# A four-layer convolution kernel: the channel mix as 64-row matmuls, and a place in the tick for each engine's part of a stage

## The chip, the core and the metric

One core of a Trainium2 chip runs the whole program. Five engines take part, each with its own queue in program order: TensorE (PE in the profile; its weight loads are the row PEld), VectorE (DVE), ScalarE (ACT), and SyncE (SP), which issues most DMA transfers; GpSimd is idle. The metric is device time in microseconds, the median of several executions. Before the change it is 2977.2 us (three runs, 2973.15 to 2978.07).

## What is computed

The input x is 4 images of 64 channels of 256 x 256, f32. Layers 0, 1 and 3 are long convolutions, written in the reference with FFTs; the filter of a channel is an outer product of a column filter and a row filter, so that the kernel does each layer as two triangular Toeplitz matmuls (along rows, then along columns) and a residual sum with a bias. Layer 2 is a Haar transform, a channel mix with thresholds, and the inverse transform:

```
k = einsum('ijk,imk->ijmk', hx, hy)            # layers 0, 1, 3: separable filters
out = irfft2(rfft2(x) * rfft2(k)) + x * bias

f1 = haar2d(x)                                  # layer 2
acc = 0
for i in range(2):
    f3 = f1 * v[i]
    f4 = einsum('bchw,oc->bohw', f3, conv_w[i]) # 64 channels to 64
    acc += sign(f4) * relu(abs(f4) - tau[i])
y = haar2d(acc, inverse=True) + x
```

## The kernel before

An image b passes through three parts, and the parts of neighbouring images overlap. `convolutions` takes a channel at a time: layer 0 and layer 1 (four products called pa and py; `contract`, L187 to L191, makes each of four matmuls), the residual sums on VectorE (L212), the pairs of the Haar transform (L257, L258), its other levels (L269, L270, four channels at once), a split of the result into two parts (L280 on ScalarE, L281 on VectorE) and a matmul for the column transform (`down`, L288), whose result ScalarE copies out (L296) and a DMA writes to DRAM as `coef`. `mixing` reads `coef` back with channels on partitions, 64 groups g for an image. `inverse` takes a channel at a time again: a copy out of z (L396), row matmuls (pw, L403, L404), a split (L406, L407), a column matmul (pu, L416), sums (L420 to L424), and layer 3. One channel in three has its layer 3 put off to the last image's mixing stage, where no channels of a next image are left (`convolution`, tile v).

What the change touches most is `mixing`. The tile f has 128 partitions: two coefficient rows r of 64 channels each. A group needs four stationary blocks of f (q and h, two each). The moving operand wb has 128 rows and 256 columns and is block-diagonal: rows 0 to 63 hold the 64 x 128 weights in columns 0 to 127, rows 64 to 127 hold them in columns 128 to 255, and the rest is zero (memset at L153, DMAs at L155). So `mix` issues 4 matmuls of 128 x 128 by 128 x 256 for a group (L340); their result px is two PSUM banks of 16 pieces of 64 columns. Each piece has a scale of its own: VectorE scales the first 16 - n_act pieces in one instruction (L357), ScalarE the other n_act with one instruction each (L359); n_act is 12, and 6 for the last image. `shrink` takes magnitude and sign on ScalarE (L365, L366) and subtracts the threshold on VectorE (L367); `signed` (L372) and `add` (L376) end the group on VectorE and write z. PSUM tiles px, and the SBUF tiles f4 and mag, have two buffers each; f has three.

The order of the work is a list of events: `at(tick, place, run, unit)`; the list is sorted by tick and place, and each event then emits its instructions. A tick has one group of `mixing`, or one channel of `inverse`. `spread` lays the 64 channels of the next image over the ticks of a mixing stage and a few before and after. A Tile scheduler then lays out each engine's queue, guided by that order.

Of the kernel before, what the change touches and what calls it, by code (L numbers as in the profile page):

```python
# [17 lines left out]
P = 128  # L18
# [3 lines left out]
BUFS = {"res": 1, "y": 3, "co": 2}  # L22

# [14 lines left out]
def conv_seq_kernel(ctx, tc, x, fz, fw, bias, decay, haar, haar_row, factors, vt, taut, wmix, out):  # L38
# [33 lines left out]
    wb = const.tile([P, 2, P], F32, name="wb")  # L72
# [3 lines left out]
    z = zpool.tile([P, 2, S, C], F32, name="z")  # L76
# [10 lines left out]
    room = z.rearrange("p h r c -> p (h r c)")  # L87
# [60 lines left out]
    def constants():  # L148
        signs = part(P)
        nc.sync.dma_start(hbt, haar[0])  # L150
        nc.sync.dma_start(signs, haar[1])
        nc.sync.dma_start(hrow, haar_row)
        nc.vector.memset(wb, 0.0)  # L153
        for r in range(2):
            nc.sync.dma_start(wb[r * C : (r + 1) * C, r, :], wmix)  # L155
        nc.scalar.copy(hb, signs)
        nc.scalar.copy(hbr, hbt)
# [35 lines left out]
    def first(b, st, key, layer, new):  # L193
        def run(c):
            s = st[c]
            ps = bank(f"p{new}_{b}_{c}")
            contract(ps, s[key], s[layer][:, 0, :])
            a = io.tile([P, 2, S], F32, name=f"{new}_{b}_{c}", tag="mid")
            nc.scalar.copy(a, ps)  # L199
            s[new] = a  # L200

        return run

    def second(b, st, key, layer, res, new, tag, ahead=None):
        def run(c):
            s = st[c]
            if ahead is not None:
                s[ahead] = toeplitz(ahead, c, f"t{ahead}_{b}_{c}")
            ps = bank(f"p{new}_{b}_{c}")
            contract(ps, s[key], s[layer][:, 1, :])  # L210
            y = io.tile([P, 2, S], F32, name=f"{new}_{b}_{c}", tag=tag, bufs=BUFS[tag])
            nc.vector.scalar_tensor_tensor(y, s[res], bsb[:, layer, c : c + 1], ps, ALU.mult, ALU.add)  # L212
            s[new] = y

        return run

    def butterfly(b):

        d = mx.tile([P, 2, C], F32, name=f"bfly_{b}", tag="mag")
        nc.vector.tensor_sub(d, z[:, :, 0, :], z[:, :, 1, :])  # L220
        nc.vector.tensor_add(z[:, :, 0, :], z[:, :, 0, :], z[:, :, 1, :])
        nc.vector.tensor_copy(z[:, :, 1, :], d)
# [5 lines left out]
    def at(tick, place, run, unit):  # L228
        events.append((tick, place, len(events), run, unit))

    def stream(stages, ticks):

        for unit, tick in enumerate(ticks):
            for s, stage in enumerate(stages):
                if stage is not None:
                    at(tick + s, -s, stage, unit)

    def convolutions(b, ticks, in_parts=(), border=None):
# [12 lines left out]
        last_second = second(b, st, "a1", 1, "y0", "y1", "res")  # L251

        def pairs(c):
            last_second(c)
# [21 lines left out]
        def split(c):  # L276

            w = parts[c] = mx.tile([P, 2, 2, S], F32R, name=f"sp_{b}_{c}", tag="sp", bufs=1)
            t = sd[:, c % 8].rearrange("p k e w -> p k (e w)")
            nc.scalar.copy(w[:, 0], t)  # L280
            nc.vector.tensor_tensor(w[:, 1], t, w[:, 0].bitcast(F32), ALU.subtract)  # L281

        def down(c):
# [7 lines left out]
            else:  # L291
                nc.tensor.matmul(
                    ps.rearrange(flat), hbt, sd[:, c % 8].rearrange("p k e w -> p (k e w)"), start=True, stop=True
                )
            t = io.tile([P, 2, S], F32, name=f"co_{b}_{c}", tag="co", bufs=BUFS["co"])
            nc.scalar.copy(t, ps)  # L296
            nc.sync.dma_start(coef[b][:, c].rearrange("k p w -> p k w"), t)

        stream(
            [load, first(b, st, "x", 0, "a0"), second(b, st, "a0", 0, "x", "y0", "y", ahead=1), first(b, st, "y0", 1, "a1"), pairs],  # L300
            ticks,
        )
        for c, tick in enumerate(ticks):

            at(tick + 4, 3, store, c)
        for n in range(C // 4):
            end = ticks[4 * n + 3] + 4
            for s, steps in enumerate([(1,), (2, 4), (8, 16, 32, 64)]):
                at(after(end + 1 + s, n), 1, levels(steps), n)
            for j in range(4):  # L310
                if 4 * n + j in in_parts:
                    at(after(end + 3 + j, n), 2, split, 4 * n + j)
                at(after(end + 4 + j, n), 2, down, 4 * n + j)
        return after(ticks[-1] + 11, C // 4 - 1)

    def mixing(b, start, n_act):
# [18 lines left out]
        def mix(g):  # L335
            f = st[g]["f"]
            ps = psx.tile([P, 2, 2, S], F32, name=f"px_{b}_{g}", tag="mix")
            for q in range(2):
                for h in range(2):
                    nc.tensor.matmul(  # L340
                        ps[:, h, q, :],
                        f[:, q, h * P : (h + 1) * P],
                        wb.rearrange("p r n -> p (r n)"),
                        start=True,
                        stop=True,
                    )
            if g == 0:

                one, two = ps[:, :, 0, :P], ps[:, :, 0, P:]
# [4 lines left out]
            f4 = mx.tile([P, 16, C], F32, name=f"f4_{b}_{g}", tag="f4")  # L354
            px = ps.rearrange("p h q (r i o) -> p (h q r i) o", r=2, i=2)
            n = 16 - n_act
            nc.vector.tensor_tensor(f4[:, :n], px[:, :n], over(g, 0, n), ALU.mult)  # L357
            for j in range(n, 16):
                nc.scalar.mul(f4[:, j], px[:, j], scale(g, 0)[:, j : j + 1])  # L359
            st[g]["f4"] = f4  # L360

        def shrink(g):
            f4 = st[g]["f4"]
            mag = mx.tile([P, 16, C], F32, name=f"mag_{b}_{g}", tag="mag")
            nc.scalar.activation(mag, f4, AF.Abs)  # L365
            nc.scalar.activation(f4, f4, AF.Sign)  # L366
            nc.vector.tensor_sub(mag, mag, over(g, 1, 16))  # L367
            st[g]["mag"] = mag
# [5 lines left out]
        def add(g):  # L374
            parts = st.pop(g)["mag"].rearrange("p (h r i) o -> p h r i o", h=2, i=2)
            nc.vector.tensor_add(z[:, :, 4 * g : 4 * g + 4, :], parts[:, :, :, 0, :], parts[:, :, :, 1, :])  # L376

        for g in range(S // 4):
            at(start + g - 2, 0, load, g)

            for s, (place, stage) in enumerate([(-2.5, mix), (-3.5, shrink), (-4.1, signed), (-4.2, add)]):
                at(start + g + s, place, stage, g)

    def inverse(b, start, put_off):
# [3 lines left out]
        def fetch(c):  # L390
# [5 lines left out]
            nc.scalar.copy(a, z[:, :, :, c].rearrange("p h (i k) -> p h k i", k=2))  # L396
            st[c] = {"r": r, "z": a}

        def rows(c):
# [5 lines left out]
            w = mx.tile([P, 2, 2, 2, P], F32R, name=f"w_{b}_{c}", tag="f4")  # L405
            nc.scalar.copy(w[:, 0], ps)  # L406
            nc.vector.tensor_tensor(w[:, 1], ps, w[:, 0].bitcast(F32), ALU.subtract)  # L407
            st[c]["w"] = w
            if c not in put_off:
                st[c][2] = toeplitz(2, c, f"t2_{b}_{c}")  # L410

        def cols(c):
            ps = psm.tile([P, 2, 2, P], F32, name=f"pu_{b}_{c}", tag="mm")
            flat = "p m e w -> p (m e w)"
            for i in range(2):
                nc.tensor.matmul(  # L416
                    ps.rearrange(flat), hb, st[c]["w"][:, i].rearrange(flat), start=(i == 0), stop=(i == 1)
                )
            t = io.tile([P, 2, 2, P], F32, name=f"t_{b}_{c}", tag="res", bufs=BUFS["res"])
# [7 lines left out]
        ends = last(b, st)  # L427
        for c in range(C):

            at(start + c, -1, fetch, c)  # L430
            at(start + c + 1, -9, rows, c)
            at(start + c + 2, -8, cols, c)
            if c in put_off:
                at(start + c + 3, -5, lambda c: nc.scalar.dma_start(late[b, c], st.pop(c)["u"]), c)
            else:
                for s, stage in enumerate(ends):
                    at(start + c + 3 + s, s - 7, stage, c)

    def last(b, st):
        return [  # L440
            first(b, st, "u", 2, "a3"),
            second(b, st, "a3", 2, "u", "y3", "co"),
# [3 lines left out]
    def convolution(which, ticks):  # L446

        for (b, c), tick in zip(which, ticks):
# [7 lines left out]
            for s, stage in enumerate([load, *last(b, st)]):  # L456
                at(tick + s, -s, stage, c)
# [21 lines left out]
    for tick, do in enumerate([constants, None, None, *three[:-1], *tables()], 4):  # L479
        if do is not None:  # L480
            at(tick, 3, lambda unit, do=do: do(), 0)
# [5 lines left out]
    for b in range(B):  # L487
        mixing(b, start, 12 if b + 1 < B else 6)
# [11 lines left out]
    for _, _, _, stage, unit in sorted(events, key=lambda e: e[:3]):  # L500
# [110 lines left out]
```

## Time and profile before

| | |
|---|---|
| median of the runs | 2977.2 us |
| the profiled execution: its time | 2975.2 us |
| its span on the core | 2973.4 us |
| busy in the span: PE, PEld | 2913.8 us (98%), 2615.1 us (88%) |
| busy in the span: DVE, ACT | 2545.5 us (86%), 2156.9 us (73%) |
| granted TensorE clock | 1.0 |
| DMA | 649.73 MB, mean 219 GB/s |

From the first to the last matmul of the mix (L340), the four mixing stages run from 453.5 to 860.1 us, 1092.1 to 1532.6, 1765.9 to 2206.2 and 2436.2 to 2707.5. Between them lie the inverse stages. Busy time is the union of an engine's instructions; a matmul's end is modelled, and matmuls overlap, so that the start-to-start times of matmuls tell their cost and not the lengths of the records. An f32 matmul appears as two records, each with a weight load of its own: the 1024 matmuls of L340 are 2048 records.

### The profile page before, as it was taken

What the parts mean: (1) busy time and instruction counts of PE and PEld (TensorE: products, weight loads), DVE (VectorE), ACT (ScalarE), POOL (GpSimd) and SP (SyncE); (2) the same over time, 40 slices, a digit from 0 to 9 for tenths busy, and PEclk for the clock granted to TensorE, in tenths of its full rate; (3) what the DMA queues carried; (4) which work ended last, traced back from release to release, by engine and by line L of the source; (5) the groups of instructions that cost most, each with busy time, mean ns of one, the idle gap of its engine ahead of it and who ended that gap; (6) DMA issues with size and microseconds to landing.
All of it is one profiled execution on the core that took longest, in us unless ns stands there. A gap on an engine that the chain in (4) does not pass through costs nothing. (4 is left out here: it accounts for less than half of the span.)

```text
span 2973.4 us, 52066 instructions
## 1 busy us (share of the span) xinstructions
PE 2913.8 (98%) x16950; PEld 2615.1 (88%) x16950; DVE 2545.5 (86%) x4571; ACT 2156.9 (73%) x5014; POOL 0.2 (0%) x4
## 2 busy tenths in 40 slices
PE   8999999999999999999999999999999999999999
PEld 6898988888888898888888988888888988888998
DVE  5766768999998879999989879999998889998776
ACT  2333338999986758889986668989986768887554
POOL 0000000000000000000000000000000000000000
PEclk9999999999999999999999999999999999999999
DMA  5877777666667876776777876777777878777676
GB/s 159 247 237 226 229 228 212 203 202 207 207 196 244 250 217 200 208 216 204 208 219 244 250 225 197 209 210 211 207 216 237 256 236 235 233 230 217 212 212 186
DMA packets 562497, 649.73 MB, mean 219 GB/s; under 512 B 44369, under 2 KB 447412, under 8 KB 562100
## 3 DMA queue, kind: packets, MB, share of 16 engines
q1 hardware_dynamic: 482996, 562.07, 64.8%
q10 hardware_dynamic: 79232, 84.34, 8.0%
q8 instruction: 137, 2.24, 0.3%
q14 instruction: 132, 1.08, 0.1%
HBM read 426.77 MB, written 219.48 MB: 217 GB/s over the span
## 5 line engine op out<-in xcount | busy, mean ns | idle before, releaser
L190 PE MATMUL py<-t,a 128*128 128x256 f32 x3072 | 919.0, 381 | 8.9 <-ACT a L199 5.5
L199 ACT COPY a<-pa 128x512 f32<-128x512 f32 x768 | 477.2, 621 | 387.9 <-PE pa L191 357.2
L359 ACT ACTIVATE f<-px,vt 128x64 f32<-128x64 f32 x2688 | 582.3, 358 | 143.5 <-DVE f L357 143.4
L191 PEld LDWEIGHTS py<-t,a 128*128 128x128 f32 x3072 | 583.4, 190 | 79.3
L191 PE MATMUL py<-t,a 128*128 128x128 f32 x3072 | 590.0, 274 | 0.0
L190 PEld LDWEIGHTS py<-t,a 128*128 128x128 f32 x3072 | 500.4, 191 | 50.9 <-ACT a L199 12.4
L340 PE MATMUL px<-wb,f 128*128 128x256 f32 x2048 | 488.2, 380 | 4.9 <-ACT f L359 4.9
L340 PEld LDWEIGHTS px<-wb,f 128*128 128x128 f32 x2048 | 369.5, 190 | 47.0 <-ACT f L359 6.7
L367 DVE TENSOR_TENSOR mag<-mag,vt 128x1024 f32<-128x1024 f32 x256 | 312.4, 1220 | 28.3 <-ACT mag L365 26.9
L190 PE MATMUL pa<-t,y 128*128 128x256 f32 x1024 | 311.6, 386 | 22.4 <-DVE y L212 20.3
L406 ACT CAST w<-pw 128x512 fp32r<-128x512 f32 x256 | 150.2, 587 | 227.0 <-PE pw L404 218.9
L372 DVE SCALAR_TENSOR_TENSOR mag<-mag,f 128x1024 f32<-128x1024 f32 x256 | 311.7, 1218 | 1.9
L190 PE MATMUL pa<-t,x 128*128 128x256 f32 x1024 | 305.9, 380 | 0.4 <-issue 0.4
L365 ACT ACTIVATE mag<-f 128x1024 f32<-128x1024 f32 x256 | 293.7, 1147 | 11.0 <-DVE z L376 8.8
L366 ACT ACTIVATE f<-f 128x1024 f32<-128x1024 f32 x256 | 285.2, 1114 | 3.0
L396 ACT COPY zc<-z 128x512 f32<-128x512 f32 x256 | 282.0, 1103 | 0.7 <-ACT w L406 0.4
L281 DVE TENSOR_TENSOR sp<-sd,sp 128x512 fp32r<-128x512 f32 x256 | 176.1, 688 | 91.4 <-ACT sp L280 90.2
L190 PE MATMUL pa<-t,u 128*128 128x256 f32 x772 | 232.8, 383 | 2.9 <-PE pu L416 1.6
L420 DVE SCALAR_TENSOR_TENSOR t<-r,pu 128x512 f32<-128x512 f32 x256 | 174.9, 683 | 60.4 <-PE pu L416 57.0
L212 DVE SCALAR_TENSOR_TENSOR y<-x,bsb,py 128x512 f32<-128x512 f32 x256 | 190.1, 742 | 37.9 <-PE py L191 36.1
L212 DVE SCALAR_TENSOR_TENSOR y<-y,bsb,py 128x512 f32<-128x512 f32 x256 | 190.0, 742 | 34.2 <-PE py L191 33.1
L191 PEld LDWEIGHTS pa<-t,x 128*128 128x128 f32 x1024 | 194.6, 190 | 26.3
(67 smaller groups left out, 4458.9 us busy)
## 6 DMA issues: line engine op xcount, KB each, us to landing
t<-pad SPq DMA_DIRECT2D x768, 256.0 KB, 3.9
x<-in_x SPq DMA_DIRECT2D x256, 256.0 KB, 3.6
keep<-sd SPq DMA_DIRECT2D x256, 256.0 KB, 2.9
coef<-co SPq DMA_DIRECT2D x256, 256.0 KB, 3.3
f<-coef SPq DMA_DIRECT2D x256, 256.0 KB, 3.2
r<-keep SPq DMA_DIRECT2D x256, 256.0 KB, 3.3
out_y<-y ACTq DMA_DIRECT2D x256, 256.0 KB, 3.6
late<-u ACTq DMA_DIRECT2D x63, 256.0 KB, 2.9
```

Source lines behind the costliest of these rows:

```text
L190: nc.tensor.matmul(ps[:, m, :], src[:, 0, m * P : (m + 1) * P], t[:, ::-1], start=True, stop=False)
L191: nc.tensor.matmul(ps[:, m, P:], src[:, 1, m * P : (m + 1) * P], t[:, : P - 1 : -1], start=False, stop=True)
L199: nc.scalar.copy(a, ps)
L212: nc.vector.scalar_tensor_tensor(y, s[res], bsb[:, layer, c : c + 1], ps, ALU.mult, ALU.add)
L281: nc.vector.tensor_tensor(w[:, 1], t, w[:, 0].bitcast(F32), ALU.subtract)
L340: nc.tensor.matmul(ps[:, h, q, :], f[:, q, h * P : (h + 1) * P], wb.rearrange("p r n -> p (r n)"), start=True, stop=True,)
L359: nc.scalar.mul(f4[:, j], px[:, j], scale(g, 0)[:, j : j + 1])
L365: nc.scalar.activation(mag, f4, AF.Abs)
L366: nc.scalar.activation(f4, f4, AF.Sign)
L367: nc.vector.tensor_sub(mag, mag, over(g, 1, 16))
L372: nc.vector.scalar_tensor_tensor(mag, mag, 0.0, st[g]["f4"], ALU.max, ALU.mult)
L396: nc.scalar.copy(a, z[:, :, :, c].rearrange("p h (i k) -> p h k i", k=2))
```

## The change

Seven things are edited.

- wb loses its zeros: it is 128 x 128, with the 64 x 128 weights twice, on partitions 0 to 63 and on 64 to 127. `mix` issues 8 matmuls for a group with 64 contraction rows and 128 moving columns, alternately on rows 0 to 63 and rows 64 to 127, the two halves into two different PSUM banks. The built program has 2048 such matmuls in place of 1024, with the tile size 64 x 128 and the tile positions (0, 0) and (64, 0).
- The pieces of px now stand in the order r, h, q, i, and the tables of scales, the layout of z, `butterfly`, `add` and the copy out of z (256 B between elements in place of 512 B) follow.
- n_act is 14 for the first image, and stays 12, 12 and 6 for the others.
- Each stage is cut by engine: a product and the copy or sum after it, `split` and `rest`, `down` and `away`, `rows` and `halves`, `cols` and `join`, and in `mixing` the scaling (VectorE's, and two halves of ScalarE's), `size`, `sign` and `shrink`.
- `at(time, run, unit)` takes one number; the table PLACE gives each part its offset from the unit's tick, with a second set (prefix l) for the last image's mixing.
- The second residual sum and the pairs of layer 1 are events of their own (4.429 and 4.639); the threshold steps (`shrink` 1.777, `signed` 2.802, `add` 3.331) get places of their own too.
- The load of f is placed 0.977 ticks before the group's tick, where it was 2 ticks before.

```diff
+N_ACT = (14, 12, 12, 6)
+PLACE = {
...
+    "y0": 2.571,
+    "y0 sum": 2.571,
...
+    "mix load": -0.977,
+    "mix": 0.536,
+    "scaled": 0.583,
+    "scaled too": 0.583,
+    "scaled rest": 0.584,
+    "size": 1.468,
+    "sign": 1.476,
+    "shrink": 1.777,
+    "signed": 2.802,
+    "add": 3.331,
...
-    wb = const.tile([P, 2, P], F32, name="wb")
+    wb = const.tile([P, P], F32, name="wb")
-    z = zpool.tile([P, 2, S, C], F32, name="z")
+    z = zpool.tile([P, 2, 2, P, C], F32, name="z")
...
-        nc.vector.memset(wb, 0.0)
         for r in range(2):
-            nc.sync.dma_start(wb[r * C : (r + 1) * C, r, :], wmix)
+            nc.sync.dma_start(wb[r * C : (r + 1) * C], wmix)
...
-    def at(tick, place, run, unit):
-        events.append((tick, place, len(events), run, unit))
+    def at(time, run, unit):
+        events.append((time, len(events), run, unit))
...
         def mix(g):
             f = st[g]["f"]
-            ps = psx.tile([P, 2, 2, S], F32, name=f"px_{b}_{g}", tag="mix")
-            for q in range(2):
-                for h in range(2):
-                    nc.tensor.matmul(
-                        ps[:, h, q, :],
-                        f[:, q, h * P : (h + 1) * P],
-                        wb.rearrange("p r n -> p (r n)"),
-                        start=True,
-                        stop=True,
-                    )
+            ps = psx.tile([P, 2, 2, 2, P], F32, name=f"px_{b}_{g}", tag="mix")
+            for h in range(2):
+                for q in range(2):
+                    for r in range(2):
+                        rows = slice(r * C, (r + 1) * C)
+                        nc.tensor.matmul(
+                            ps[:, r, h, q, :], f[rows, q, h * P : (h + 1) * P], wb[rows], start=True, stop=True
+                        )
...
-            px = ps.rearrange("p h q (r i o) -> p (h q r i) o", r=2, i=2)
+            st[g]["px"] = ps.rearrange("p r h q (i o) -> p (r h q i) o", i=2)
+
+        def scaled(g):
+            px, n = st[g]["px"], 16 - n_act
+            nc.vector.tensor_tensor(st[g]["f4"][:, :n], px[:, :n], over(g, 0, n), ALU.mult)
+
+        def scaled_too(g, half):
+            px, f4 = st[g]["px"], st[g]["f4"]
+            for j in range(16 - n_act + half * (n_act // 2), 16 - (1 - half) * (n_act - n_act // 2)):
+                nc.scalar.mul(f4[:, j], px[:, j], scale(g, 0)[:, j : j + 1])
+
+        def size(g):
+            mag = st[g]["mag"] = mx.tile([P, 16, C], F32, name=f"mag_{b}_{g}", tag="mag")
+            nc.scalar.activation(mag, st[g]["f4"], AF.Abs)
+
+        def sign(g):
+            nc.scalar.activation(st[g]["f4"], st[g]["f4"], AF.Sign)
...
-            parts = st.pop(g)["mag"].rearrange("p (h r i) o -> p h r i o", h=2, i=2)
-            nc.vector.tensor_add(z[:, :, 4 * g : 4 * g + 4, :], parts[:, :, :, 0, :], parts[:, :, :, 1, :])
+            parts = st.pop(g)["mag"].rearrange("p (s q i) o -> p s q i o", q=2, i=2)
+            rows = z.rearrange("p r h i c -> p (r h) i c")[:, :, 2 * g : 2 * g + 2, :]
+            nc.vector.tensor_add(rows, parts[:, :, :, 0, :], parts[:, :, :, 1, :])
...
-            nc.scalar.copy(a, z[:, :, :, c].rearrange("p h (i k) -> p h k i", k=2))
+            nc.scalar.copy(a, z[:, :, :, :, c].rearrange("p k h i -> p h k i"))
...
-        mixing(b, start, 12 if b + 1 < B else 6)
+        mixing(b, start, N_ACT[b])
```

## The prediction

> **What bounds the kernel now.** The page names PE as the chain's main engine, but its busy shares are means over unlike stages. So I first read the busy times cut at the stages: image 0's first convolutions, the four mixing stages (the third equals the second to 0.2 us and is left out), the last inverse stage, and a piece of the last mixing.
>
> ```profile
> core 0: us, PE busy (x) PEld busy (x) DVE busy (x) ACT busy (x) POOL busy (x), PEclk, DMA share, GB/s
> 60.00:450.00 390.00, 385.11 (x2276) 348.76 (x2275) 272.99 (x593) 146.63 (x270) 0.00 (x0) 1.00 0.78 231
> 455.00:860.00 405.00, 395.56 (x2171) 349.90 (x2171) 386.89 (x668) 374.99 (x1077) 0.00 (x0) 1.00 0.68 204
> 1092.00:1532.00 440.00, 434.27 (x2428) 389.47 (x2427) 407.76 (x716) 386.39 (x1092) 0.00 (x0) 1.00 0.71 208
> 2436.00:2707.00 271.00, 265.85 (x1434) 236.40 (x1433) 264.30 (x309) 233.17 (x554) 0.00 (x0) 1.00 0.79 234
> 2725.00:2955.00 230.00, 229.93 (x1476) 212.07 (x1475) 164.93 (x306) 135.51 (x186) 0.00 (x0) 1.00 0.69 210
> 2600.00:2650.00 50.00, 49.23 (x267) 43.89 (x267) 49.80 (x58) 45.07 (x109) 0.00 (x0) 1.00 0.80 235
> ```
>
> Outside the mixing stages PE alone is full (99 to 100%), and the change takes no matmul out there. In the mixing stages three engines are nearly full together: 98.7, 92.7 and 87.8% in the second. The waits inside that stage say which one sets the pace (engine, line, waited for: us, times, longest):
>
> ```profile
> DVE y L212 <- PE py L191: 11.3, 15, 1.2
> ...
> PE pa L190 <- DVE y L212: 4.9, 7, 1.7
> ...
> ACT f L359 <- DVE f L357: 45.9, 45, 2.5
> ```
>
> PE waits 4.9 us of 440; ScalarE waits for VectorE's scaling, VectorE for PE. The end is set by PE, with VectorE 6% behind. Last, the group rows of the mix and the order of time around one group of it, and around a start with nothing preloaded (start, us, engine, line):
>
> ```profile
> L340 PE MATMUL px<-wb,f 128*128 128x256 f32 x2048 | 488.2, 380 | 4.9 <-ACT f L359 4.9
> L357 DVE TENSOR_TENSOR f<-px,vt 128x256 f32<-128x256 f32 x192 | 80.4, 419 | 0.5 <-PE px L340 0.5
> L357 DVE TENSOR_TENSOR f<-px,vt 128x640 f32<-128x640 f32 x64 | 52.3, 817 | 1.5
> ```
>
> ```profile
> 1007.33 0.30 PEld L403 LDWEIGHTS pw<-hrow,zc 128*128 128x128 f32 x2
> ...
> 1007.67 0.30 PEld L403 LDWEIGHTS pw<-hrow,zc 128*128 128x128 f32 x2
> ...
> 1304.71 1.89 PE L340 MATMUL px<-wb,f 128*128 128x256 f32 x8
> ...
> 1306.43 0.59 PE L190 MATMUL py<-t,a 128*128 128x256 f32 x2
> ...
> 1307.49 2.56 ACT L359 ACTIVATE f<-px,vt 128x64 f32<-128x64 f32 x12 [0.38 <-DVE f L357]
> ...
> 2553.31 1.99 PE L340 MATMUL px<-wb,f 128*128 128x256 f32 x8 [0.69 <-ACT f L359]
> ```
>
> A group of the mix costs PE 1306.43 - 1304.71 = 1.72 us: 8 records of 0.215. Between the two load lines at 1007.33 and 1007.67 lie three records of 128 columns, so one costs 0.34/3 = 0.113 us, whether its load or its stream sets that.
>
> **The change, part by part.** The span has 64 groups in each of four stages. I divide by the groups each window holds (L340's records in it: 505, 509, 509, by 8: 63.1, 63.6, 63.6). Per group, in us:
> first stage: 6.42, of it PE 6.27, DVE 6.13, ACT 5.94; second and third: 6.92, of it 6.83, 6.41, 6.08; last: 4.26, of it 4.18, 4.16, 3.67.
>
> *The mix.* 16 records of 128 columns on 64 rows replace 8 of 256. The trace has no pair on two row halves, so I bound. One after another they cost 16 x 0.113 = 1.81 us. If the halves run side by side, in loads and streams both, half: 0.90. To this come the two borders of a group, where the array passes from 128-row to 64-row work and back. The least is nothing, as between L340 and L190 now. The most is a full drain and an exposed start: a record outlasts its slot by 0.380 - 0.215 = 0.165, and the mix at 2553.31, which began with its load, ran 1.99 against 1.89, 0.10 more; 0.27 a border, 0.53 a group. Side by side thus costs 0.90 to 1.43, and I take the middle, 1.17: 0.55 less than now (0.29 to 0.82). I take side by side because the built program addresses the halves separately and gives each half its own PSUM bank, so nothing that the program declares chains one half to the other.
>
> Two rules bear on this. The Trainium skill, TensorE: Matmul & The Clock Gate, section LDWEIGHTS, speaks against the change: a load's time goes by its columns and not by its rows, P/1.2 ns, so a 64-row load is no cheaper; as an estimate 16 x 107 ns = 1.71 us a group if loads queue, which by itself would cancel the gain. TensorEngine Tiling (Array Packing), Key Properties, says that different tiles load and multiply in parallel, which would give 0.86, and that a change of tiling mode drains TensorE, which is on the side of my upper border cost. The 0.113 agrees with the first for full-height loads; no run here shows the rest.
>
> *What that is worth.* In the second and third stages PE falls from 6.83 to 6.28 and VectorE's 6.41 becomes the most. How near can a group's time come to it? In the last stage, where VectorE is full already, it is busy 264.30 of 271 us, 97.5%. 6.41/0.975 = 6.57, 0.35 below 6.92; 64 groups in two stages: **-45 us**. Ends: VectorE at the 99.6% of 2600 to 2650 gives 6.44, -61; half of the gap kept in waits between ScalarE and VectorE gives -20.
>
> *n_act 14 in the first stage.* VectorE's L357 goes from 256 to 128 elements, at (817 - 419)/(640 - 256) = 1.04 ns each: -0.13, to 6.00. ScalarE gets two more instructions at (2.56 - 0.36)/11 = 0.20 each (0.36: L359's mean of 358 ns): 5.94 + 0.40 = 6.34, which is 98.8% of 6.42. So ScalarE takes PE's place, and I take **0**. Ends: ScalarE packs better and VectorE decides, 6.00/0.975 = 6.15, -17; ScalarE at 97.5%, 6.50, +5.
>
> *The last stage.* VectorE's 4.16/0.975 is today's 4.26: **0**, and -5 if it reaches 99.6% throughout.
>
> *The places.* I laid the two programs' queues side by side. In the convolution and inverse stages PE's queue, matmul by matmul, and ScalarE's read alike in the stretches I compared; VectorE's differ by a neighbour here and there. In mixing the second image's groups keep their sequence (PE: mix, py, pa, pz, py, pa; VectorE: scale, sign, sum, add, sum, split, pairs, subtract). SP's loads of f, t and v stand in the same sequence in the last mixing stage, though the table puts f's load later, so no transfer is moved past another there. So I cost the table at 0; what hides its small shifts is VectorE's slack outside mixing (272.99 of 390 us busy). If a group lost one 0.4 us instruction's wait on VectorE to it, that would be 0.4 x 128 = 51 us in the second and third stages; the like gain is inside the -61 above.
>
> *Layout of z.* The copy out of z (L396, 1103 ns) may change with its step; it lies in the inverse stages, where ScalarE is busy 133 of 202 us (59% in the last) and PE is full: 0 up or down, unless it grew by over 1.0 us of a channel's 3.2 (202 us by 64). The memset saved is 0.3 us.
>
> Sum: 2973.4 - 45 = 2928 us of span; the median runs stand 3.8 us above that span (2977.2), so **2932 us**, with 2894 (-83: -61, -17, -5) to 2962 (-15: -20, +5) as this case's own range.
>
> **Rivals.** *The halves don't run side by side* (the slower side). Place: `mix`, in the four mixing stages. Price: 1.81 plus 0 to 0.53 for 1.72, that is 0.09 to 0.62 more on PE, the engine that sets the pace (the last stage's PE is 98% busy, so it pays too): 256 x 0.09 = +23 to 256 x 0.62 = +159, so 3000 to 3136. It decides from the point where a group costs PE over 1.72 us. For it: the loads, doubled in number, have at 0.113 each no room under 0.9 us of streams. Against: separate halves and banks.
>
> *The relieved PE finds the others in its old rhythm.* ScalarE's 45.9 us of waits for the scaling, and 12 instructions of 2.56 us behind each, make a chain from PE to VectorE to ScalarE and back to VectorE. If each group is held by that chain and not by busy time, the second and third stages stay at 6.92, and the first at 6.42 to 6.50: 2977 to 2982. Against it: in the last stage the same chain runs in 4.26 us.
>
> *The borders cost more than a drain.* If each border cost 0.41 us, the gain of 0.82 would be gone: no change. That is the point where the forecast turns without the halves failing; it joins the second rival.
>
> **How the numbers follow.** Forecast 0.65, halves in a row 0.23, no effect 0.12. The measurement can tell about 0.2%, 6 us, from no change. Faster: 0.65 + 0.03 of the no-effect case = 0.68; same 0.09; slower 0.23. The predicted time is the likeliest's, 2932. Range: below 2890 I leave 0.04; up to 3040 lie the no-effect case and some 0.3 of the slower one, so 0.16 are left above. Its low end is the forecast's best, its high end is a step of 0.25 us a group on PE.
>
> **What would show it.** Right: records of 128 columns at L418 of the new kernel, a group of 16 within about 1.2 us; VectorE 96% or more of the second and third mixing stages, each near 420 us; the first stage near 405 with ScalarE at 98%; convolution and inverse stages unchanged within 2 us. Wrong: 16 records at 0.11 in a row (PE per group 1.8 or more), or PE idle in mixing while neither VectorE nor ScalarE is over 95%, or a change outside the mixing stages.

## The result and the profile after

The changed kernel takes 2976.35 us (median of 12 runs, 2973.54 to 2979.29), the kernel before 2976.16 us (12 runs, 2971.97 to 2978.81). The ratio is 1.0003, 95% interval 0.9995 to 1.0011: no change that can be told, where 2932 us were forecast.

The busy times of the profiled execution of the changed kernel (span 2973.9 us), cut at the same stretches as before (engine busy us and number of records, then granted clock, DMA share, GB/s):

```profile
core 0: us, PE busy (x) PEld busy (x) DVE busy (x) ACT busy (x) POOL busy (x), PEclk, DMA share, GB/s
60.00:450.00 390.00, 384.38 (x2276) 348.80 (x2275) 273.10 (x593) 146.79 (x270) 0.00 (x0) 1.00 0.77 231
455.00:860.00 405.00, 376.80 (x2673) 327.00 (x2671) 380.39 (x669) 396.45 (x1201) 0.00 (x0) 0.99 0.68 203
1092.00:1532.00 440.00, 414.39 (x2922) 364.63 (x2922) 406.98 (x716) 387.32 (x1092) 0.00 (x0) 0.99 0.70 208
2436.00:2707.00 271.00, 245.06 (x1978) 213.37 (x1978) 265.51 (x317) 235.09 (x556) 0.00 (x0) 0.99 0.81 238
2725.00:2955.00 230.00, 229.94 (x1476) 212.06 (x1475) 165.63 (x306) 135.82 (x187) 0.00 (x0) 1.00 0.70 211
```

PE is relieved in every mixing stage: by 19 us in the first, 20 in the second, 21 in the last. In the second stage nothing takes its place: VectorE was busy for 407.8 us of 440 before and is busy for 407.0 now. TensorE has been given 20 us, and it spends them idle. From the first group's start to the last group's start, as stages are given everywhere below, the four took 405.0, 439.0, 438.8 and 269.8 us before and take 405.7, 441.1, 440.7 and 266.9 now.

The mix itself did what it should. TensorE's timeline around one group (start, us, engine, line), and the mix that followed the one at 1304.71 in the kernel before:

```profile
1301.98 0.38 PE L248 MATMUL pa<-t,y 128*128 128x128 f32 x2
1302.29 1.16 PE L418 MATMUL px<-wb,f 64*128 64x128 f32 x16
1303.38 0.70 PE L247 MATMUL py<-t,a 128*128 128x256 f32 x2
...
1309.28 1.16 PE L418 MATMUL px<-wb,f 64*128 64x128 f32 x16
```

```profile
1312.13 1.89 PE L340 MATMUL px<-wb,f 128*128 128x256 f32 x8
```

Sixteen records take 1303.38 - 1302.29 = 1.09 us, 0.068 each, where one after another at 0.113 would take 1.81. The two halves run side by side: the records start in pairs, one on each half, 0.007 us apart, and a pair every 0.11 us. A full group, one in which PE never waits, now takes 1309.28 - 1302.29 = 6.99 us; before it took 7.43. So the mix costs 1.72 - 0.44 = 1.28 us, borders included.

What PE and VectorE wait for in the second stage, 1092 to 1532 us (engine, line, waited for: us, times, longest):

```profile
ACT f L438 <- DVE f L433: 48.2, 55, 3.3
...
PE pa L247 <- DVE y L278: 21.0, 17, 2.7
DVE sp L342 <- ACT sp L337: 13.7, 17, 1.1
DVE y L278 <- PE py L248: 8.3, 5, 2.6
...
PE py L247 <- ACT a L261: 4.0, 6, 0.7
...
DVE mag L449 <- ACT mag L442: 2.9, 7, 0.4
```

PE's wait for VectorE's residual sum has gone from 4.9 to 21.0 us, and 4.0 for ScalarE's copy have come: together the 20 us it was given. VectorE's own waits have moved and not shrunk: before, 11.3 for PE's py, 10.9 for ScalarE's magnitude and 2.6 for its cast; now 8.3, 2.9 and 13.7.

Where a full group is held shows in the two queues of one such group, VectorE first, then ScalarE:

```profile
1305.39 0.42 DVE L433 TENSOR_TENSOR f<-px,vt 128x256 f32<-128x256 f32 x1
...
1309.92 0.69 DVE L342 TENSOR_TENSOR sp<-sd,sp 128x512 fp32r<-128x512 f32 x1 [1.06 <-ACT sp L337]
1310.53 0.42 DVE L315 TENSOR_TENSOR sd<-y 128x256 f32<-128x256 f32 x1
1310.86 0.42 DVE L316 TENSOR_TENSOR sd<-y 128x256 f32<-128x256 f32 x1
1311.20 1.22 DVE L449 TENSOR_TENSOR mag<-mag,vt 128x1024 f32<-128x1024 f32 x1
1312.33 0.42 DVE L433 TENSOR_TENSOR f<-px,vt 128x256 f32<-128x256 f32 x1
```

```profile
1305.84 2.56 ACT L438 ACTIVATE f<-px,vt 128x64 f32<-128x64 f32 x12 [0.38 <-DVE f L433]
1308.22 0.66 ACT L261 COPY a<-pa 128x512 f32<-128x512 f32 x1
1308.69 0.68 ACT L360 COPY co<-pz 128x512 f32<-128x512 f32 x1
1309.16 0.72 ACT L337 CAST sp<-sd 128x512 fp32r<-128x512 f32 x1
```

Read the starts as one loop: VectorE's scaling at 1305.39, ScalarE's twelve scalings from 1305.84, two copies, the cast at 1309.16, VectorE's L342 at 1309.92, then in its queue the pairs, the threshold, and the next scaling at 1312.33. No step of it waits for anything outside it, and it lasts 6.94 us. PE's 6.99 and this loop are equal to within 0.05, so as long as the queues keep this order a full group can't be shorter than some 6.95, whatever is taken from PE next. VectorE has one gap in it, 1.06 us.

The Haar level steps (L327, L328) have to fit into that gap, and they don't. They come four channels at a time, 14 instructions of 0.17 to 0.69 us each, and fall on two or three groups. In such a group, still VectorE:

```profile
1320.98 0.41 DVE L315 TENSOR_TENSOR sd<-y 128x256 f32<-128x256 f32 x1
1321.32 0.41 DVE L316 TENSOR_TENSOR sd<-y 128x256 f32<-128x256 f32 x1
1321.65 0.60 DVE L328 SCALAR_TENSOR_TENSOR sd<-sd 128x256 f32<-128x256 f32 x1
1322.17 0.41 DVE L433 TENSOR_TENSOR f<-px,vt 128x256 f32<-128x256 f32 x1
```

Every start here follows the one before at once, and so it goes from 1316.10 to 1330.27; scaling to scaling takes 1329.86 - 1322.17 = 7.69 us. The groups of the stage repeat with eight channels, which take nine groups. Once the stage has settled, their times show the exchange: before, six of 7.43, then some 6.8, 4.35 and 6.5, 62.1 to 62.4 in all; now four of 6.99, one of 7.7, one of 8.4 to 11.0, one of 6.5 to 7.5, 4.1 and 6.4, 62.1 to 63.6 in all. What full groups gain, the groups with level steps give back. VectorE is busy for 58.9 to 59.1 us of such nine groups in both kernels, 95% of them and not the 92.7% of the whole stage. What it waits for in nine groups, before (1409 to 1471 us) and after (1410 to 1472):

```profile
DVE y L212 <- PE py L191: 1.7, 2, 1.2
DVE mag L367 <- ACT mag L365: 0.7, 1, 0.7
DVE sp L281 <- ACT sp L280: 0.2, 1, 0.2
```

```profile
DVE sp L342 <- ACT sp L337: 2.3, 3, 1.1
DVE mag L449 <- ACT mag L442: 0.4, 1, 0.4
```

Of some 62 us VectorE stood 1.7 for PE. That wait is gone, and the wait for ScalarE's cast, which closes the loop, has grown by 2.1: the sum is 2.6 before and 2.7 after. In other settled periods waits for transfers in front of the level steps come on top, up to 1.6 us now and 0.2 before.

TensorE's granted clock does not explain the result. It was 1.0 through all mixing stages before; now it falls to half for 3.4 us ten times in them (0.50 in the profile's window 1325.2 to 1328.5 us). In the second and third stages four settled groups hold such a stretch, each just after PE had waited 2.0 to 2.7 us; they take 10.3 to 11.0 us, where the groups in the same place without one take 8.4 to 9.3. Over the twelve runs the mean clock lay between 0.994 and 0.999, and the time did not follow it: 2973.54 us at 0.999, 2979.29 at 0.998, 2974.11 at 0.995.

### The profile page after: what moved, and what is told of

Same layout as the page of the kernel before. It is cut to its first block, busy times and chain, and to the rows that moved or that the text cites. A ratio compares the mean times of both kernels' runs of the same rounds, so it can differ in the third digit from the quotient of the medians.

```text
span 2973.9 us, 56224 instructions
## 1 busy us (share of the span) xinstructions
PE 2824.2 (95%) x18998; PEld 2514.2 (85%) x18998; DVE 2525.8 (85%) x4570; ACT 2184.5 (73%) x5142; POOL 0.2 (0%) x4
## 5 line engine op out<-in xcount | busy, mean ns | idle before, releaser
L247 PE MATMUL py<-t,a 128*128 128x256 f32 x3072 | 946.7, 390 | 50.7 <-ACT a L261 45.1
L438 ACT ACTIVATE f<-px,vt 128x64 f32<-128x64 f32 x2816 | 616.2, 381 | 116.6 <-DVE f L433 111.8
L248 PEld LDWEIGHTS py<-t,a 128*128 128x128 f32 x3072 | 585.8, 191 | 80.4
L247 PEld LDWEIGHTS py<-t,a 128*128 128x128 f32 x3072 | 484.1, 191 | 112.6 <-ACT a L261 64.0
L449 DVE TENSOR_TENSOR mag<-mag,vt 128x1024 f32<-128x1024 f32 x256 | 313.1, 1223 | 12.6 <-ACT mag L442 11.3
L418 PE MATMUL px<-wb,f 64*128 64x128 f32 x4096 | 305.7, 287 | 11.3 <-ACT f L438 11.3
L418 PEld LDWEIGHTS px<-wb,f 64*128 64x128 f32 x4096 | 254.3, 189 | 45.8 <-ACT f L438 12.8
L342 DVE TENSOR_TENSOR sp<-sd,sp 128x512 fp32r<-128x512 f32 x256 | 176.5, 689 | 122.9 <-ACT sp L337 122.2
L278 DVE SCALAR_TENSOR_TENSOR y<-x,bsb,py 128x512 f32<-128x512 f32 x256 | 190.7, 745 | 40.7 <-PE py L248 40.3
L248 PEld LDWEIGHTS pa<-t,y 128*128 128x128 f32 x1024 | 196.6, 192 | 27.2
```

Of the source, the lines that this page charges most:

```text
L247: nc.tensor.matmul(ps[:, m, :], src[:, 0, m * P : (m + 1) * P], t[:, ::-1], start=True, stop=False)
L248: nc.tensor.matmul(ps[:, m, P:], src[:, 1, m * P : (m + 1) * P], t[:, : P - 1 : -1], start=False, stop=True)
L418: nc.tensor.matmul(ps[:, r, h, q, :], f[rows, q, h * P : (h + 1) * P], wb[rows], start=True, stop=True)
```

## The experiments

Eighteen runs, each against the kernel before on the same chip. "Stages" are the four mixing stages in us, from group start to group start.

### The two halves of the change by themselves

`mix_only` is the kernel before with the 64-row mix and its layouts; `places_only` is the kernel after with the old mix and n_act 12 in the first image.

```diff
 mix_only
-                    nc.tensor.matmul(ps[:, h, q, :], f[:, q, h * P : (h + 1) * P], wb.rearrange("p r n -> p (r n)"), ...)
+                        nc.tensor.matmul(ps[:, r, h, q, :], f[rows, q, h * P : (h + 1) * P], wb[rows], ...)
```

> The kernel before, with the 64-row mix and the layouts that go with it alone: old places, n_act 12, 12, 12, 6. Theory A (PE's relief is real, about 0.5 us a group, but VectorE's Haar-level steps come in bursts, and groups with a burst become VectorE-bound): no gain here either, 2960 to 2985 us, with plain groups of the second mixing stage at 6.9 to 7.1 us and some groups over 8 us. Rival B (the mix gains what was forecast and the new places or n_act 14 lose it again): 2925 to 2950.

> The changed kernel with the old mix (block-diagonal weights, 4 matmuls of 256 columns a group), the old layouts and n_act 12 in the first image; the new places stay. Theory A: 2970 to 2985, plain groups at 7.43 us as before the change. Rival B: the places cost what the mix gains, 3005 to 3030.

`mix_only`: 2992.14 us, ratio 1.0057 (1.0042 to 1.0072); stages 404.8, 445.3, 444.0, 272.8. `places_only`: 2974.73 us, 0.9998 (0.9988 to 1.0007); stages 403.9, 439.0, 438.9, 271.1. With the old mix the table of places is worth nothing, as forecast. With the new mix it is worth 16 us (with n_act 14, for which `after_nact12` below shows 2 us at most): without it the shorter mix makes the kernel slower. Neither theory had that. In `mix_only` full groups also take 6.99 us, and the groups with level steps 7.2 to 9.0; the scheduler had laid VectorE's queue out differently, with one of the two batches of 14 level steps as 3, 8 and 3 over three groups, where the kernel before has 3, 7 and 4. No run shows that this is what costs the 16 us.

### VectorE's level steps left out

The levels after the first are left out in both kernels, 28 VectorE instructions per eight channels, so the coefficients are not the reference's.

```diff
-                for step in steps:
+                for step in ():
```

> The kernel before without the Haar levels after the first (448 pairs of VectorE instructions are left out, so the coefficients are not the transform's). Theory A: plain groups stay PE-bound at 7.43 us, so little is won: 2945 to 2975. Rival C (a chain of hand-overs between PE, VectorE and ScalarE sets the pace of a group, not busy time): the same, no more than 10 us under before.

> The changed kernel without the Haar levels after the first, left out as in before_nolev. Theory A: all full groups run at PE's 6.99 us; 9 groups take about 58.3 us in place of 62.1, so 50 us less in the second and third stages and some 20 in the first: 2890 to 2925, at least 40 us under before_nolev. Rival C: 2955 to 2975, as far from the changed kernel as before_nolev is from the one before.

`before_nolev`: 2936.04 us, 0.9871 (0.9854 to 0.9887); stages 395.8, 430.1, 430.2, 269.9. `after_nolev`: 2913.68 us, 0.9792 (0.9777 to 0.9807); stages 402.9, 420.6, 420.6, 266.8. Now the change is worth 22 us. Theory A had expected 40 or more between the two, and `before_nolev` came out below both of its ranges. The second and third stages fall by 9.5 us each, while PE's busy time in the second falls by 20 (429.5 us of its 430 before, 409.7 of 420 after): half of what is taken from PE comes off the time. 300 us of the second stage, `before_nolev` and then `after_nolev`:

```profile
1100.00:1400.00 300.00, 299.48 (x1687) 270.82 (x1687) 250.28 (x371) 275.37 (x777) 0.00 (x0) 1.00 0.71 211
```

```profile
1100.00:1400.00 300.00, 292.96 (x2096) 257.52 (x2095) 252.98 (x377) 279.73 (x789) 0.00 (x0) 1.00 0.71 216
```

The third busy time, VectorE's, is 250 to 253 us, its load down by a tenth. In the kernel before PE is full at 99.8% and sets the pace; in the kernel after it is not (97.7%), although no engine is fuller. VectorE's waits in these 300 us, in the same order:

```profile
DVE y L212 <- PE py L191: 35.2, 37, 1.6
DVE sp L281 <- ACT sp L280: 7.9, 10, 1.3
```

```profile
DVE sp L342 <- ACT sp L337: 34.3, 31, 1.6
...
DVE y L278 <- PE py L248: 4.8, 4, 1.9
```

VectorE waits 30.4 us less for PE and 26.4 more for ScalarE's cast, the step that closes the loop. So about half of the relief is lost to the loop even where VectorE has time to spare.

### More or fewer scalings on ScalarE

```diff
-N_ACT = (14, 12, 12, 6)
+N_ACT = (12, 12, 12, 6)    after_nact12
+N_ACT = (12, 14, 14, 8)    after_nact_more
```

> The changed kernel with n_act 12 in the first image, as before the change. Theory A (VectorE's bursts of level steps bind the groups): the first stage stays at 400 to 412 us, the whole 2965 to 2985. Rival D (ScalarE with 14 pieces, busy 396 of 405 us in the first stage, eats that stage's gain): the first stage falls to 390 or less, the whole to 2945 to 2962.

> The changed kernel with n_act 12, 14, 14, 8: work goes from VectorE to ScalarE where VectorE is full. Theory A: VectorE has 0.13 us less a group in the last three stages; the last stage falls by 8 us, the second and third by 3 to 5 each: 2952 to 2968. If ScalarE binds instead (0.4 us more a group): 2972 or more.

`after_nact12`: 2978.3 us, 1.0009 (1.0000 to 1.0019); stages 406.2, 441.9, 439.6, 267.5. `after_nact_more`: 3020.35 us, 1.0154 (1.0139 to 1.0169); stages 409.3, 445.1, 445.3, 288.7. Two scalings more on ScalarE take 0.13 us from VectorE's instruction and add 0.4 us to ScalarE's part of the loop: 6.94 + 0.27 = 7.21. Theory A expected shorter stages. The second and third get longer by 4 to 5 us, and three of the nine groups there now take 7.1 to 7.2 us, though PE's work in them is 6.99 as before. VectorE in one of them:

```profile
1316.55 0.28 DVE L433 TENSOR_TENSOR f<-px,vt 128x128 f32<-128x128 f32 x1
...
1321.35 0.69 DVE L342 TENSOR_TENSOR sp<-sd,sp 128x512 fp32r<-128x512 f32 x1 [1.46 <-ACT sp L337]
...
1323.77 0.28 DVE L433 TENSOR_TENSOR f<-px,vt 128x128 f32<-128x128 f32 x1
```

Scaling to scaling is 7.22 us, the length that the loop should have, and its gap is the wait for the cast. So the loop holds these groups, with PE's work as before and VectorE's smaller. The last stage gets longer by 22 us in another way: between 2500 and 2700 us PE waits 18.4 us, where it waited 6.7, for ScalarE's scalings to give px back. In the first stage 14 or 12 make no difference.

### The level steps spread or moved

`even` leaves the levels out and gives VectorE instead three further 128x256 instructions with each channel's pairs: 1.0 us a channel, near what the levels cost, but evenly. `two` does the levels for two channels at a time. `poolsub` gives L327, one of each two level instructions, to GpSimd (L269 in the kernel before).

```diff
 after_even
-            nc.vector.tensor_add(t[:, :, 0, :], v[:, :, :, 0], v[:, :, :, 1])
-            nc.vector.tensor_sub(t[:, :, 1, :], v[:, :, :, 0], v[:, :, :, 1])
+            for again in range(5):
+                nc.vector.tensor_tensor(t[:, :, again % 2, :], v[:, :, :, 0], v[:, :, :, 1], ...)
 after_two
-                t = sd[:, n % 2 * 4 : n % 2 * 4 + 4]
+                t = sd[:, n % 4 * 2 : n % 4 * 2 + 2]
 after_poolsub
-                    nc.vector.tensor_sub(odd, even, odd)
+                    nc.gpsimd.tensor_sub(odd, even, odd)
```

> The changed kernel without the level steps, but with three more VectorE instructions of 256 elements in each channel's pairs (5 in place of 2, the last write standing), 1.0 us a channel against the 0.96 us that the level steps take start to start; the levels after the first are left out of the result. Theory A (bursts): VectorE's work is as much as before but even, so the second and third stages come near after_nolev's 420.6: 420 to 430 each, the whole 2912 to 2940. Theory F (VectorE's whole load, in whatever shape, binds with the waits around it): 2960 to 2980.

> The kernel before with the same even work in place of the level steps. Theory A: PE binds, as in before_nolev (2936): 2934 to 2952. Theory F: 2960 to 2980.

> The changed kernel with the level steps on two channels at a time in place of four: the same result, twice the instructions of half the elements, half the burst twice as often. VectorE's own work grows by about 0.1 us a channel. Theory A: the second and third stages fall to 425 to 436, the whole 2935 to 2962. Theory F: 2975 to 3000.

> The kernel before with the level steps on two channels at a time. Theory A: 2945 to 2970, at least 8 us above after_two. Theory F: 2975 to 3000.

> The changed kernel with the first instruction of each level step (the difference, L327) on GpSimd, which was idle; VectorE loses 0.6 us a channel. Theory A: the second and third stages fall towards the 420.6 us that they took with no levels at all: 425 to 433 each, the whole 2930 to 2958. Rival C (a chain of hand-overs): no change, 2970 to 2980. Rival E (GpSimd and VectorE hinder each other, so that VectorE's instructions grow): 2975 or more, with VectorE's threshold instructions over 1.25 us.

> The kernel before with the same move to GpSimd. Theory A: PE binds the plain groups at 7.43 us; the stages fall towards the 430 us that they took without levels, and not below: 2940 to 2962, and 10 to 20 us slower than after_poolsub. Rival E: 2975 or more.

| run | us | ratio (interval) | stages |
|---|---|---|---|
| after_even | 2957.9 | 0.9941 (0.9927 to 0.9956) | 402.2, 437.5, 437.5, 266.9 |
| before_even | 2950.36 | 0.9917 (0.9901 to 0.9934) | 392.2, 432.2, 432.1, 269.9 |
| after_two | 2996.78 | 1.0072 (1.0057 to 1.0088) | 405.0, 449.4, 450.3, 267.7 |
| before_two | 2989.64 | 1.0050 (1.0035 to 1.0065) | 402.5, 449.7, 448.1, 269.9 |
| after_poolsub | 3052.95 | 1.0259 (1.0244 to 1.0274) | 422.5, 457.1, 457.1, 266.9 |
| before_poolsub | 3071.58 | 1.0323 (1.0308 to 1.0339) | 426.3, 462.8, 464.3, 269.8 |

`after_even` lies between its two theories: spread evenly, the load still costs 44 us against `after_nolev`, of the 63 us that the levels cost. A full group of `after_even`, VectorE:

```profile
1302.19 0.42 DVE L433 TENSOR_TENSOR f<-px,vt 128x256 f32<-128x256 f32 x1
...
1306.73 0.69 DVE L342 TENSOR_TENSOR sp<-sd,sp 128x512 fp32r<-128x512 f32 x1 [0.48 <-ACT sp L337]
1307.34 1.43 DVE L316 TENSOR_TENSOR sd<-y 128x256 f32<-128x256 f32 x4
1308.68 1.22 DVE L449 TENSOR_TENSOR mag<-mag,vt 128x1024 f32<-128x1024 f32 x1
1309.81 0.42 DVE L433 TENSOR_TENSOR f<-px,vt 128x256 f32<-128x256 f32 x1
```

It is the same loop, now 7.62 us long, since four of the five pair instructions stand behind the cast. VectorE waits inside it for ScalarE, and PE, with 6.99 us of work, waits for VectorE's sum. Here the loop is the longest of the three. So even work is not neutral work: where it stands in the queue, it lengthens the loop. In the kernel before, whose PE takes 7.43 a full group anyway, the same load costs only 14 us against `before_nolev`, as theory A expected: the more PE is relieved, the more such a loop shows. The levels in pairs of channels cost more instructions and slow the kernel after by 20 us and the kernel before by 14, in theory F's range. The two runs with GpSimd fall in rival E's range, but its sign is missing: in `after_poolsub` the threshold instructions take 1.22 and 1.23 us, not over 1.25. In `after_poolsub` VectorE has half of the level work less, and its other half waits for it (the group of L328: busy, mean ns, idle before it):

```profile
L328 DVE SCALAR_TENSOR_TENSOR sd<-sd 128x512 f32<-128x512 f32 (+6 forms) x448 | 164.3, 367 | 206.8 <-POOL sd L327 187.8
```

Each L328 stands behind a subtraction that takes GpSimd 667 ns, where VectorE took 368. With its queue in order, all of VectorE stands there for 188 us.

### The cast taken out of the loop

```diff
-            nc.scalar.copy(w[:, 0], sd[:, c % 8].rearrange("p k e w -> p k (e w)"))
+            nc.gpsimd.tensor_copy(w[:, 0], sd[:, c % 8].rearrange("p k e w -> p k (e w)"))
```

> The cast sp (one 128x512 copy a channel) goes from ScalarE to GpSimd, which has nothing else to do there; the result is the same. ScalarE keeps its 12 scalings, sizes, signs and both copies; VectorE's work is unchanged. Theory R (the ring VectorE L433 -> ScalarE's scalings, copies and cast -> VectorE L342 -> L315 to L449 -> next L433, 6.94 us in a full group, holds the group once TensorE is relieved): the ring is cut, full groups fall to TensorE's 6.99 and the groups with level steps to VectorE's own load; the 2nd and 3rd mixing stage come to about 430 us each (from 441), the first to 400 to 405; median 2935 to 2960. Theory L (VectorE's load and the uneven place of its level steps alone set these stages, whatever ScalarE does): 2nd and 3rd stage 438 to 443, median 2968 to 2980. Should GpSimd's cast arrive later than ScalarE's did (over 1 us and in front of L342), the 2nd and 3rd stage go above 445 with the idle time ahead of L342 put down to it.

> The same move of the cast in the kernel before. Theory R: TensorE's 7.43 us in full groups hold there, not the ring; 2nd and 3rd stage 434 to 439, median 2962 to 2977, so the kernel after stands 10 us or more below it with the cast moved, where without that the two are equal. Theory L: 436 to 441 and the two kernels still within 5 us of each other.

> As after_poolcast, and 14 of the 16 scalings on ScalarE in the first three images (12 in the 2nd and 3rd before). Theory R: with the cast gone ScalarE has 0.6 us a group to take them, VectorE is relieved by some 0.13 us a group, and the 2nd and 3rd stage fall by another 2 to 6 us each; median 5 to 12 us below after_poolcast. Theory L: VectorE's relief shows alike (2 to 6 us a stage) but from the higher level, 2960 to 2970. If ScalarE's chain still counts, the stages are as long as in after_poolcast or longer, as the 14 scalings were in an earlier run with the cast on ScalarE (445 us).

`after_poolcast`: 3020.76 us, 1.0140 (1.0126 to 1.0153); stages 418.2, 452.6, 450.9, 267.0. `before_poolcast`: 3024.7 us, 1.0156 (1.0142 to 1.0170); stages 412.8, 448.8, 450.0, 269.9. `after_poolcast14`: 3032.23 us, 1.0181 (1.0167 to 1.0195); stages 416.5, 455.0, 451.3, 266.9. Both theories expected less, and 14 scalings made it 11 us longer, not shorter. (The stages went above 445 us, as the warning of a late cast had it, but VectorE waits only 0.2 us for the cast.) The waits of `after_poolcast` in the second stage:

```profile
ACT f L438 <- DVE f L433: 78.0, 51, 3.2
...
DVE mag L449 <- ACT mag L442: 18.4, 22, 1.2
...
DVE sp L342 <- POOL sp L337: 0.2, 1, 0.2
```

The wait for the cast is gone, 13.7 to 0.2 us. In its place VectorE waits for ScalarE's magnitude, 18.4 us where it waited 2.9. So this edit doesn't decide between the loop and VectorE's load: it removed one wait, lengthened another, and had a third effect, which the last batch made plain.

### VectorE relieved of an instruction outside the loop

```diff
-            nc.vector.tensor_add(rows, parts[:, :, :, 0, :], parts[:, :, :, 1, :])
+            nc.gpsimd.tensor_add(rows, parts[:, :, :, 0, :], parts[:, :, :, 1, :])
```

> The sum that writes z (L458, one 128x512 instruction of 0.69 us a group) goes from VectorE to GpSimd; the result is the same, and z is read only after the stage. VectorE's queue keeps its sequence without it. Theory L (VectorE's own load, met by an in-order hand-over with ScalarE, holds the relieved kernel): with 0.69 of its 6.4 us a group gone TensorE decides, as it did with the level steps left out (420.6 us in the 2nd and 3rd stage): 418 to 426 there, 400 to 406 in the first stage (ScalarE), 245 to 267 in the last; median 2905 to 2940. Theory R (the ring of 6.94 us alone, in which L458 has no part): full groups stay at 6.99, only groups with level steps get shorter; 430 to 437 in the 2nd and 3rd stage, median 2950 to 2970. Should GpSimd hold the buffers mag (two of them, and its instruction over 1 us), ScalarE's L442 will show waits for it and the stages are 441 or more.

> The same move of the sum in the kernel before (L376). Theory L: TensorE decides at 7.43 us in full groups, as with the level steps left out: 429 to 435 in the 2nd and 3rd stage, 395 to 400 in the first, 268 to 270 in the last; median 2932 to 2955, and the kernel after 15 us or more below it. Theory R: 434 to 440 and 2955 to 2977, and the two kernels within 10 us.

> As after_pooladd with 12 instead of 14 scalings on ScalarE in the first image. Only the first stage may change. If ScalarE holds it (L, as in the run without level steps, where it was busy 403 of 405 us), it falls by 6 to 15 us to 388 to 397; if VectorE or the ring holds it (R), it stays within 2 us.

`after_pooladd`: 3035.83 us, 1.0209 (1.0195 to 1.0223); stages 419.1, 455.4, 455.1, 271.3. `before_pooladd`: 3050.09 us, 1.0256 (1.0242 to 1.0270); stages 421.8, 460.0, 460.6, 269.5. `after_pooladd12`: 3041.71 us, 1.0232 (1.0218 to 1.0246); stages 424.4, 454.4, 454.8, 271.8. Again no theory had it, and the buffers mag are not the reason: in the second stage ScalarE never waits for GpSimd. GpSimd's timeline in `after_pooladd` (start, us):

```profile
1301.27 1.59 POOL L458 TENSOR_TENSOR z<-mag 128x512 f32<-128x512 f32 x1 [4.68 <-DVE mag L453]
1309.24 1.27 POOL L458 TENSOR_TENSOR z<-mag 128x512 f32<-128x512 f32 x1 [6.38 <-DVE mag L453]
```

And VectorE's at the same times:

```profile
1301.05 0.69 DVE L327 TENSOR_TENSOR sd<-sd 128x512 f32<-128x512 f32 x1
1301.77 1.64 DVE L328 SCALAR_TENSOR_TENSOR sd<-sd 128x512 f32<-128x512 f32 x1
...
1309.00 0.27 DVE L327 TENSOR_TENSOR sd<-sd 128x64 f32<-128x64 f32 x1
1309.30 1.33 DVE L328 SCALAR_TENSOR_TENSOR sd<-sd 128x64 f32<-128x64 f32 x1
```

L328 takes 1.64 us where it takes 0.69 elsewhere, and 1.33 where it takes 0.27: both start while GpSimd's instruction runs and end 0.55 and 0.12 us after it. Relieving VectorE by way of GpSimd therefore stretches other VectorE instructions, and the eight runs with work on GpSimd can't be read as "VectorE with less load". Summed over all VectorE instructions that overlap one of GpSimd's, against the same instruction without overlap, the stretch is 99 us in `after_pooladd`, where 175 were taken off VectorE, 28 in `after_poolcast` and 14 in `after_poolsub`. Full groups of `after_pooladd` stay at 6.99 us, but PE alone would give that too, so they don't tell the loop from PE.

No version tried here that computes the whole result beats the kernel before.

## Why the prediction was wrong

*What bounds the kernel.* PE set the pace in the groups of 7.43 us, and relieving it moved the pace elsewhere. But "VectorE 6% behind" was read from means over a stage. Once the stage has settled, VectorE was busy for 59.0 of 62.2 us and waited 1.7 for PE, which is all that a faster PE by itself could hand it. In the whole second stage that wait is 11.3 us, and it stood among the lines shown; the forecast took 22 us off the stage.

*The mix.* Right. Side by side, 1.17 us forecast with 0.90 to 1.43 as bounds, 1.28 measured, borders included. Of the two rules weighed there, the first held for a single load and not for the queue: a load record lasts 0.189 us with 64 rows and 0.190 with 128, but the 16 loads of L418 at 1302.29 span 0.97 us, less than the 1.71 that loads in a row would take. That different tiles load in parallel, as the Trainium skill, TensorEngine Tiling (Array Packing), section Key Properties, states, agrees with these rows; the 0.86 was an estimate from it. The drain that this page gives for a change of mode may be part of 1.28 - 1.09 = 0.19 us a group, within the 0.53 allowed; no run parts it from the rest.

*What that is worth.* This step failed: "How near can a group's time come to it? In the last stage, where VectorE is full already, it is busy 264.30 of 271 us, 97.5%". Forecast -45 us, measured +4 (stages +2.1 and +1.9). VectorE stayed at 92.5% of the second stage. The 97.5% came from a stage in which the loop has six scalings and neither cast, copy out nor pairs. In the second and third stages a full group did get PE's whole relief, 7.43 to 6.99 us, and came down on the loop's 6.94. The groups with level steps grew by as much, for over the nine groups VectorE had no time to give: its 1.7 us of waiting for PE became 2.1 us more of waiting for ScalarE's cast. Taking VectorE's load away does not bring the forecast back. The 420.6 us of `after_nolev` look like the forecast's "near 420", but the kernel before takes 430 with the same load, and the change is worth 9.5 us a stage there, where the forecast's own sum, with VectorE no longer in the way, would have given all of PE's relief.

*The rival that held.* "The relieved PE finds the others in its old rhythm" gave 2977 to 2982 and had 0.12 with the borders. I dismissed it because "in the last stage the same chain runs in 4.26 us"; it is not the same chain there. `after_nact_more` and `after_even` show that the loop can hold a full group (7.22 and 7.62 us), `after_nolev` that about half of PE's relief is lost to it even without level steps. The other half is lost only with the level steps, in the groups that hold them. How the lost 45 us divide between the two in the changed kernel itself was not settled: the runs that should have parted them ran into GpSimd's cost.

*n_act 14 in the first stage.* The 0 came true (405.0 to 405.7), and ScalarE is at 97.9% as forecast. But its reason is only half shown: with 12 the stage took 406.2 as well. Without the level steps the first stage takes 402.9 us with 14 and the new mix, against 395.8 with 12 and the old, and ScalarE is nearly full there (403.4 of 405 us); that the 14 scalings are the cause was not tested by itself, and in `after_pooladd12` the stage is longer with 12 (424.4 against 419.1 us).

*The last stage.* Forecast 0 to -5, measured -3 (269.8 to 266.9).

*The places.* Forecast 0. With the old mix that is right, and for the whole change it hid two terms: the mix alone +16 us, the places (with n_act 14) on top of it -16. I had compared the queues of the two finished kernels only; what the shorter mix by itself does to the scheduler's order did not come into view.

*z and the memset.* Between the stages nothing moved by more than 2.1 us, near the 2 that were forecast.

## What to carry to other kernels

When three engines are nearly full in a stage, relieving the first is worth the sum, over the unlike units of that stage, of what the next constraint leaves in each unit, and not the distance between the stage's mean loads. Ask first how long the next engine waits for the one that is relieved: here 1.7 of 62 us. Follow one unit's instructions from start to start through the in-order queues until the loop closes; its length is a bound that no busy share shows. Before forecasting from another stage's best busy share, check that the loop there has the same members.

## What the runs showed of the hardware

Row halves of TensorE: 16 f32 records of 64 rows and 128 columns, alternating between the halves and each with its own load, take 1.09 us, against 0.113 for one record on 128 rows.

GpSimd holds VectorE up when its instruction starts first. In `after_pooladd` VectorE instructions with two inputs in SBUF mostly lasted longer when they started during one of GpSimd's: L328 with 512 elements 1.65 us in 12 such cases, where it takes 0.69 alone; L327 with 64 elements 1.04 in 16 cases, alone 0.27; L449 1.55 in 34 cases, alone 1.22. Where VectorE's had started first they kept their time: 0.69 in 7 cases of L328, 0.27 in 15 of L327. L278, with one input in PSUM, stayed at 0.74 us in all 221 of its overlaps. The Trainium skill, SBUF — State Buffer, section SBUF: two separate sides, says that the two engines share a port pair, that one holds it for its whole instruction, and that a VectorE instruction with two SBUF inputs needs it against a GpSimd one that reads SBUF. These rows agree with it.
